# Edge messages of a graph layer: older messages summed in each two-pair turn, and gathers released at four points in eight units

## The chip, the cores and the metric

The kernel runs on one core of one Trainium2 chip. The metric is the device time of one execution in microseconds (us), and lower is better. A core has five engines with a queue each: TensorE (PE, matrix products; its weight loads are listed apart as PEld), VectorE (DVE), ScalarE (ACT), GpSimd (POOL) and SyncE (SP). Each engine works through its own list of instructions in order; where one needs another's result it waits for a semaphore. DMAs are started from the lists of SP, ACT and POOL.

## The reference

One layer of a graph network over 6,250 nodes with 256 features and 206,250 edges sorted by target node. Biases are left out here:

```python
h    = relu(layernorm(x))                      # node rows, 6250 x 256
e    = relu(raw @ W_e1.T) @ W_e2.T             # raw: 64 features of each edge
emb  = (e * (polarity + 0.01)) @ W_le.T
msg  = relu(h[src] + emb)                      # a gather of 256 floats for each edge
aggr = segment_sum(msg, dst)                   # sum over the edges of each target node
out  = x + relu(layernorm((h + aggr) @ W_g1.T)) @ W_g2.T
```

All of it is float32.

## The kernel before

Edges are cut into 403 blocks of 512. A block has two **units** of 256 edges, 806 in all (`NU`), and two blocks make a **pair** (`NP` = 202). `W_e2` and `W_le` are multiplied once at the start into one matrix `wc_s`, so an edge passes through two products. The steps of the edge loop, with the names and lines that the change touches:

- `first_layer(q)` (lines 278 to 311) takes pair `q`: four 64-row products of 512 columns (`pz<-raw,we_s`, line 292), two for each half `c` of the hidden features. The relu into `e1` is done by ACT (line 308, three of four) and DVE (line 305, one of four).
- `edge_part(u)` (317 to 334) takes unit `u`: four products (line 325) into one PSUM bank; DVE adds a bias and writes `msg` (line 331).
- `gather()` (627 to 639): POOL starts one indirect DMA for 128 source rows of `hb_d` into half of `hg[u]`, so there are two for each unit. There are 20 `hg` buffers (`HG`).
- `whole(u)` (677 to 690): DVE multiplies by the polarity and adds the gathered rows (line 685, two instructions), ACT does the relu (line 690). From here on `hg[u]` is a finished message; `made` counts them.
- `add_up(b)` (692 to 711): PE sums the messages of block `b` over target nodes with a 0/1 matrix `sel`, in four column strips of 32 (`pd<-hg,sel`, line 703). This frees the two `hg` buffers. `summed` counts pairs.

PSUM banks for the products come from a ring of seven (`Ring`). A product into a bank waits until the reader of what the bank held before has finished.

All engines' lists come from one Python loop that calls the steps in a fixed order (`manual_schedule`), so the order around the change is written out by hand. `forward(u)` (line 358) calls `edge_part(u)`, and after each fourth unit `turn_of` (343 to 356). In the middle of the run (`by_two`, pairs 6 to 195) only every second turn acts and does twice the work: that is the **two-pair turn** after unit 8k+1. It sums two pairs (`add_pairs`, 735), then does two `first_layer` calls and starts the loads of two more `raw` tiles. A period is thus eight units and one such turn; there are 93 full turns from unit 41 to unit 777.

Which pairs are summed is decided in `add_pairs`: a pair whose last message is older than the newest finished one, that is `4 * (summed + pairs) + 4 < made`. The first sum of a pair waits for that pair's last message (`newest`, lines 705 to 707). `whole` runs behind `edge_part` by a lag that falls by one every 44 units (`SHRINK`), from 18 to 1 (line 940). So the distance between the newest summed message and the newest finished one runs through 1, 2, 3 and 4 units as the lag falls; call this the **slack**. Over the run it is 1 or 2 in 45 of the 93 turns and 3 or 4 in the other 48.

Gathers are held back by a pace: `in_step` (646 to 652) is called after each unit and after each half of a first layer with the time that PE is assumed to need (1.754, 0.9; sums add 0.46 for a block, node work 0.81). It lets gathers go while their number times 1.288 is below the sum of these plus 6.0, and not more than the `hg` buffers allow (`4 * summed + HG` units). The first of those let go in a call waits for the PE instruction just recorded (`behind`); the others follow it in POOL's list. From unit 782 on (line 936) the gathers are only held by the buffers.

Finished nodes (128 at a time) go through the two last products, their layer norm and the output, as small steps (lines 159 to 232) spread over the units. The first of these in a node's life wait for sums that were written to DRAM and read back.

Of the kernel before, what the change touches and what calls it, by code (L numbers as in the profile page):

```python
# [36 lines left out]
NP = -(-NB // 2)  # L37
# [5 lines left out]
EDGE, LAYER, SUMS, NODES = 1.754, 0.9, 0.46, 0.81  # L43
STEP = 1.288
AFLOAT = 6.0
BANKS = 7
SHRINK = 44
RAW = 4
HG = 16 + RAW
FEW = 6  # L50
# [8 lines left out]
def group_of(b):  # L59
    return b // L  # L60
# [40 lines left out]
def gnn_kernel(ctx: ExitStack, tc: tile.TileContext, x, src_c, dst_c, dst_r, pol_c, raw_t, w_e1t, w_e2,  # L101
# [37 lines left out]
    def behind(ins, other):  # L139

        if other is not None:
            tc.add_manual_dep(ins.ins, other.ins.name, mybir.DependencyInfo(
                mybir.DependencyClass.Sync, mybir.DependencyReason.DATA), reason="one wait for several")
# [90 lines left out]
    NU = 2 * NB  # L234
    fast = ExitStack()
    fast.enter_context(tc.manual_schedule())
    with fast:
# [11 lines left out]

        banks = [psz.tile([P, 2, D], F32, name=f"pz{i}") for i in range(BANKS)]  # L250

        class Ring:
# [4 lines left out]
            def __call__(self):  # L257
                self.taken += 1
                return banks[self.taken % BANKS]

# [6 lines left out]
            def old(self):  # L267
                n = self.taken - BANKS
                return self.readers.get(n), self.writers.get(n)
# [8 lines left out]
        def first_layer(q):  # L278

            bs = [b for b in (2 * q, 2 * q + 1) if b < NB]  # L280
            if not bs:
                return
            for b in bs:
                e1[b] = e1_p.tile([P, 2, 512], F32, name="e1")
            pe, z = {}, {}
            for c in range(2):
                olds = []
                for s, b in enumerate(bs):
                    pe[s, c] = ps().rearrange("p a b -> p (a b)")
                    olds.append(ps.old())  # L290
                for s, b in enumerate(bs):
                    z[c] = nc.tensor.matmul(pe[s, c], we1_s[s * F:(s + 1) * F, c * P:(c + 1) * P],  # L292
                                            raw[q][s * F:(s + 1) * F, :], start=True, stop=True)
                    ps.wrote(z[c], len(bs) - 1 - s)
                    reader, writer = olds[s]
                    if reader is not None and writer is not None:
                        tc.declare_no_dep(z[c].ins, writer.ins, reason="the bank's reader has waited for it")
                    if s == 0:
                        for reader, _ in olds[1:]:
                            behind(z[c], reader)  # L300
                paced(LAYER, z[c])
            for c in range(2):
                for s, b in enumerate(bs):
                    if s == c == 1:
                        a = nc.vector.tensor_scalar(e1[b][:, c, :], pe[s, c], be1_s[:, c:c + 1], 0.0, op0=ALU.add,  # L305
                                                    op1=ALU.max)
                    else:
                        a = nc.scalar.activation(e1[b][:, c, :], pe[s, c], AF.Relu, bias=be1_s[:, c:c + 1])  # L308
                    behind(a, z[c])
                    ps.read(a, len(bs) * (1 - c) + len(bs) - 1 - s)  # L310
            raw.pop(q)

        def plain(u):

            return u < LEAD and u % 3 == 1

        def edge_part(u):

            nonlocal last_z
            b, v = divmod(u, 2)  # L320
            pz = ps()
            for i in range(2):
                k = (2 * v + i) * P
                for c in range(2):
                    last_z = nc.tensor.matmul(pz[:, i, :], e1[b][:, c, k:k + P], wc_s[:, c, :], start=c == 0, stop=c == 1)  # L325
            ps.wrote(last_z)
            msg[u] = msg_p.tile([P, 2, D], F32, name="msg")
            if plain(u):
                ps.read(nc.scalar.activation(msg[u], pz, AF.Copy))
            else:  # L330
                ps.read(nc.vector.tensor_add(msg[u], pz, bc_s))  # L331
            if v == 1:
                e1.pop(b)
            paced(EDGE, last_z)

        last_z = None
        sums = lambda last: None
        paced = lambda us, behind: None

        def by_two(q):  # L340
            return FEW <= q < NP - FEW
# [65 lines left out]
        with tc.tile_pool(name="p1", bufs=4) as p1, tc.tile_pool(name="p1x", bufs=11) as p1x:  # L407
# [76 lines left out]
            for k in range(len(parts) + 1):  # L484
                last = len(parts) - 1
# [20 lines left out]
                for _ in range((k > 0) + (k > 2 and k % 3 > 0)):  # L506
                    u = next(units, None)
# [37 lines left out]
        def rows_of_edges():  # L545
            nc.vector.tensor_tensor(
                rel[:, :full].rearrange("p (g k j) -> p g k j", k=L, j=S),
                dst_f[:, :full].rearrange("p (g k j) -> p g k j", k=L, j=S),
                base_b[:, :NF, :].rearrange("p g (o j) -> p g o j", o=1).to_broadcast([P, NF, L, S]), ALU.subtract)
            nc.vector.tensor_tensor(rel[:, full:], dst_f[:, full:], base_b[:, NF, :], ALU.subtract)  # L550
# [63 lines left out]
        with tc.tile_pool(name="hg", bufs=HG - RAW) as hg_p, tc.tile_pool(name="ms", bufs=4) as ms_p, \  # L614
# [5 lines left out]
            got = 2 * RAW  # L620
            acc = {}
            done = {}
            made = 0
            summed = 0
            spent = 0.0

            def gather(behind=None):

                nonlocal got
                u, i = divmod(got, 2)  # L630
                got += 1
                if i == 0:
                    hg[u] = (hx_p if u % HG < RAW else hg_p).tile([P, 2, D], F32, name="hg")
                g = nc.gpsimd.indirect_dma_start(  # L634
                    out=hg[u][:, i, :], out_offset=None, in_=hb_d,
                    in_offset=bass.IndirectOffsetOnAxis(ap=src_s[:, 2 * u + i:2 * u + i + 1], axis=0))
                if behind is not None:
                    tc.add_manual_dep(g.ins, behind.ins.name, mybir.DependencyInfo(
                        mybir.DependencyClass.Sync, mybir.DependencyReason.DATA), reason="gathers in step with PE")
# [3 lines left out]
                while got < 2 * min(NU, last):  # L643
                    gather()

            def in_step(us, behind):

                nonlocal spent
                spent += us
                while (got - 2 * RAW) * STEP < spent + AFLOAT and got < 2 * min(NU, 4 * summed + HG):  # L650
                    gather(behind)
                    behind = None

            def select(g):

                return [(g, lambda k=k: rows_of_block(g, k)) for k in range(len(blocks_of(g)))]
# [35 lines left out]
            def add_up(b, newest=()):  # L692

                nonlocal spent
                g = group_of(b)
                k = b - g * L
                if k == 0:
                    acc[g] = pd[:, g % 2, :] if g < NG - 1 else ps()[:, 0, :]
                    while rest and rest[0][0] <= g:
                        rest.popleft()[1]()  # L700
                for j in range(S):
                    m = hg[2 * b + j // 2]
                    z = nc.tensor.matmul(acc[g][j * W:(j + 1) * W, :], sel[g][:, k * S + j, :], m[:, j % 2, :],  # L703
                                         start=k == 0, stop=b == blocks_of(g)[-1])
                    if j == 0:
                        for other in newest:
                            behind(z, other)
                hg.pop(2 * b)
                hg.pop(2 * b + 1)
                spent += SUMS  # L710
                return g if b == blocks_of(g)[-1] else None
# [23 lines left out]
            def add_pairs(last=False):  # L735

                nonlocal summed
                whole_groups = []
                pairs = 0
                while summed + pairs < NP and min(4 * (summed + pairs) + 4, NU) < made + last:  # L740
                    pairs += 1
                for _ in range(pairs):
                    newest = done.get(4 * summed + 3, ())
                    for b in (2 * summed, 2 * summed + 1):
                        if b < NB:
                            whole_groups.append(add_up(b, newest))
                            newest = ()
                            if b % L == 0 and group_of(b) + 2 < NG:
                                rest.extend(select(group_of(b) + 2))
                    summed += 1  # L750

                for g in whole_groups:
                    keep(g)
# [160 lines left out]
            gathers(RAW + 1)  # L914
            sums = add_pairs
            paced = in_step
            def strips():
                rows_of_edges()
                rest.extend(select(0) + select(1))
# [44 lines left out]
            before, last = ending[-2], ending[-1]  # L964
# [201 lines left out]
```

## Time and profile before

| what | value |
|---|---|
| time, median of 3 runs | 2580.09 us (2572.7 to 2583.99) |
| the profiled execution: time, span | 2579.07 us, 2577.4 us |
| mean granted TensorE clock in it | 0.946 |
| PE busy | 2314.6 us, 90% of the span |
| PE weight loads busy | 1634.7 us, 63% |
| DVE busy | 1613.4 us, 63% |
| ACT busy | 1019.3 us, 40% |
| POOL busy | 1618.9 us, 63% |

The profile lists instructions in groups by source line and shape, as `line engine operation out<-in xcount | busy us, mean ns of one | idle us of the engine just before them, and what ended that idle time`. A product in float32 shows as two rows of PE and two of PEld. "issue" means that the profile shows nothing that the engine waited for; "remote" means a semaphore whose source it could not name. In rows of the waits the three numbers are the idle time in total, the number of times, and the longest, in us. In rows of time windows the columns are the length, then the busy time of PE, PEld, DVE, ACT and POOL with the number of instructions, the granted PE clock, the DMA engines' share and GB/s.

### The profile page before, as it was taken

The numbers are of one execution on the slowest core, as the hardware profiler recorded it, in microseconds if no ns is written. First come the engines' busy times: TensorE is split into PE (matmuls) and PEld (weight loads), VectorE is DVE, ScalarE is ACT, GpSimd is POOL, SyncE is SP. The second block draws the span as 40 slices with busy tenths as digits, with TensorE's granted clock in tenths as the row PEclk, the third lists the DMA queues.
The fourth block names the chain that finished last, engine by engine and source line by source line (L and its number), as shares of the span: only waits on it lengthen the run. The fifth ranks groups of instructions, "written<-read, shape, count | busy, mean of one in ns | idle before, by whom it ended". The sixth has DMA issues, their size and how long they took to land.

```text
span 2577.4 us, 36784 instructions
## 1 busy us (share of the span) xinstructions
PE 2314.6 (90%) x11940; PEld 1634.7 (63%) x11940; DVE 1613.4 (63%) x3705; ACT 1019.3 (40%) x1804; POOL 1618.9 (63%) x1675
## 2 busy tenths in 40 slices
PE   9988999989989998988888999998989899888968
PEld 6666666666657666666666666665667566666646
DVE  7866666666656665665656565665656566656636
ACT  7443434343334434343433333343434334333423
POOL 6666666666656666666666666666666666666661
PEclk9899999999989999999999999999999999999989
DMA  9443444434444434443444444444434445443441
GB/s 306 139 135 113 121 123 131 130 115 133 125 118 136 132 112 129 129 132 112 125 125 122 132 134 118 122 130 129 136 115 117 129 123 148 117 132 114 121 119 47
DMA packets 176430, 330.30 MB, mean 128 GB/s; under 512 B 39055, under 2 KB 98280, under 8 KB 176232
## 3 DMA queue, kind: packets, MB, share of 16 engines
q0 software_dynamic: 77376, 211.39, 29.2%
q1 hardware_dynamic: 97556, 113.22, 13.7%
q10 hardware_dynamic: 1300, 3.28, 0.4%
q8 instruction: 95, 1.56, 0.2%
q14 instruction: 103, 0.84, 0.1%
HBM read 293.92 MB, written 33.82 MB: 127 GB/s over the span
## 4 chain that ended last, share of the span: by engine, by line
PE 81%; issue 8%; DVE 5%; another core or an unknown queue 3%; ACT 3%; DMA 0%; ACTq 0%; DVEq 0%
PE pz L325 50%; PE pz L292 17%; PE pd L703 8%; DVE hg L685 2%; PE pz L181 2%; PE pz L212 2%; DVE msg L331 1%; ACT e L308 1%; ACT hg L690 1%; PE pz L166 0%; PE pz L199 0%; DVE st L151 0%; DVE sel L663 0%; ACT xt L440 0%
## 5 line engine op out<-in xcount | busy, mean ns | idle before, releaser
L634 POOL DMA_INDIRECT hg<-hb_d,src_s x1604 | 1574.1, 981 | 897.5 <-issue 520.0
L325 PE MATMUL pz<-wc_s,e 128*128 128x256 f32 x6448 | 1494.5, 388 | 15.5 <-issue 13.0
L325 PEld LDWEIGHTS pz<-wc_s,e 128*128 128x128 f32 x6448 | 1236.4, 194 | 281.6 <-ACT e L308 65.1
L690 ACT ACTIVATE hg<-hg 128x512 f32<-128x512 f32 x805 | 507.5, 630 | 988.5 <-DVE hg L685 800.8
L331 DVE TENSOR_TENSOR msg<-pz,bc_s 128x512 f32<-128x512 f32 x799 | 545.0, 684 | 404.9 <-remote 163.5
L685 DVE SCALAR_TENSOR_TENSOR hg<-msg,pol_s,hg 128x256 f32<-128x256 f32 x1612 | 694.7, 476 | 0.4
L292 PE MATMUL pz<-raw,we_s 64*128 64x512 f32 x1612 | 487.4, 696 | 141.6 <-ACT e L308 86.8
L305 DVE TENSOR_SCALAR e<-pz,vecs 128x512 f32<-128x512 f32 x201 | 150.8, 750 | 504.6 <-PE pz L292 358.4
L308 ACT ACTIVATE e<-pz,vecs 128x512 f32<-128x512 f32 x605 | 367.0, 692 | 202.3 <-PE pz L292 147.9
L292 PEld LDWEIGHTS pz<-raw,we_s 64*128 64x128 f32 x1612 | 177.0, 210 | 395.6 <-issue 232.8
L703 PE MATMUL pd<-hg,sel 128*32 128x256 f32 x3216 | 259.2, 388 | 88.1 <-issue 81.1
L703 PEld LDWEIGHTS pd<-hg,sel 128*32 128x32 f32 x3216 | 110.9, 109 | 216.6 <-issue 163.4
L718 ACT ACTIVATE ms<-pd 128x256 f32<-128x256 f32 x66 | 25.3, 383 | 318.8 <-remote 133.2
L663 DVE SCALAR_TENSOR_TENSOR sel<-iota_w,zero_c,rel 128x128 f32<-128x128 f32 x403 | 137.8, 342 | 0.0
L181 PE MATMUL pz<-wg_s,hT 128*128 128x256 f32 (+1 forms) x196 | 52.8, 393 | 2.6 <-ACT hg L690 2.1
L212 PE MATMUL pz<-wg_s,nT 128*128 128x256 f32 (+1 forms) x196 | 50.8, 382 | 2.0 <-ACT nT L203 1.8
L181 PEld LDWEIGHTS pz<-wg_s,hT 128*128 128x128 f32 (+1 forms) x196 | 37.7, 195 | 10.4 <-ACT hg L690 2.5
L212 PEld LDWEIGHTS pz<-wg_s,nT 128*128 128x128 f32 (+1 forms) x196 | 36.8, 190 | 8.7 <-ACT nT L203 2.7
L444 POOL TENSOR_TENSOR hb<-xt,rows_b 128x256 f32<-128x256 f32 (+1 forms) x49 | 34.1, 728 | 10.5 <-ACT xt L440 4.4
L203 ACT ACTIVATE nT<-pz,vecs 128x128 f32<-128x128 f32 (+1 forms) x98 | 38.7, 444 | 2.6 <-PE pz L199 2.4
L800 DVE TENSOR_TENSOR stb<-stb,ab 128x256 f32<-128x256 f32 x94 | 38.7, 411 | 0.0
L230 DVE SCALAR_TENSOR_TENSOR xt<-xt,zero_c,rows_b 128x128 f32<-128x128 f32 (+1 forms) x98 | 33.5, 343 | 0.0
(108 smaller groups left out, 376.2 us busy)
## 6 DMA issues: line engine op xcount, KB each, us to landing
raw<-in_raw_t_dram SPq DMA_DIRECT2D x202, 256.0 KB
hg<-hb_d,src_s POOLq DMA_INDIRECT x1604
sum_d<-zrow SPq DMA_DIRECT2D x94, 128.0 KB
ab<-sum_d SPq DMA_DIRECT2D x94, 128.0 KB
sum_d<-ms SPq DMA_DIRECT2D x264, 32.0 KB
hb_d<-hb SPq DMA_DIRECT2D x12, 512.0 KB
xt<-in_x_dram SPq DMA_DIRECT2D x48, 128.0 KB
out_dram<-ot SPq DMA_DIRECT2D x48, 128.0 KB
```

What stands on the lines that cost most here:

```text
L181: z = nc.tensor.matmul(ph[:n, 0, :], aT[:, c, :n], wg1_s[:, c, :], start=c == 0 and not bias_by_pe, stop=c == 1)
L212: z = nc.tensor.matmul(po[:n, 0, :], nT[:, c, :n], wg2_s[:, c, :], start=c == 0, stop=c == 1)
L292: z[c] = nc.tensor.matmul(pe[s, c], we1_s[s * F:(s + 1) * F, c * P:(c + 1) * P], raw[q][s * F:(s + 1) * F, :], start=True, stop=True)
L305: a = nc.vector.tensor_scalar(e1[b][:, c, :], pe[s, c], be1_s[:, c:c + 1], 0.0, op0=ALU.add, op1=ALU.max)
L308: a = nc.scalar.activation(e1[b][:, c, :], pe[s, c], AF.Relu, bias=be1_s[:, c:c + 1])
L325: last_z = nc.tensor.matmul(pz[:, i, :], e1[b][:, c, k:k + P], wc_s[:, c, :], start=c == 0, stop=c == 1)
L331: ps.read(nc.vector.tensor_add(msg[u], pz, bc_s))
L634: g = nc.gpsimd.indirect_dma_start(out=hg[u][:, i, :], out_offset=None, in_=hb_d, in_offset=bass.IndirectOffsetOnAxis(ap=src_s[:, 2 * u + ...
L663: nc.vector.scalar_tensor_tensor(sel[g][:, k * S:(k + 1) * S, :], iota_w.rearrange("p (o w) -> p o w", o=1).to_broadcast([P, S, W]), zero_ ...
L685: product = nc.vector.scalar_tensor_tensor(hg[u][:, i, :], m[:, i, :], pol_s[:, 2 * u + i:2 * u + i + 1], hg[u][:, i, :], op0=ALU.mult, op ...
L690: done[u] = product, nc.scalar.activation(hg[u], hg[u], AF.Relu)
L703: z = nc.tensor.matmul(acc[g][j * W:(j + 1) * W, :], sel[g][:, k * S + j, :], m[:, j % 2, :], start=k == 0, stop=b == blocks_of(g)[-1])
```

## The change

Two things change, both in the middle of the run.

**Sums.** `add_pairs` takes a pair only if it is two units older than before (`LATER`), except near the end and in the last call. The slack of 1, 2, 3, 4 units becomes 5, 6, 3, 4: in 45 of the 93 turns the pair summed second is the one that used to be summed first in the next place, so all sums there come one pair later; in the other 48 turns the same pairs are summed as before. A turn still has two pairs.

**Gathers.** `in_step` lets gathers go only when its caller says `gate`. That is so after units 3, 5 and 7 of eight, and after the first half of the first `first_layer` in the two-pair turn (the third of its eight products is then next). To the allowance half of half a period's assumed time is added (`HALF / 2`, 5.27). In the order of the built program a period's 16 gathers stand at four places, with some 5, 5, 3 and 3 or 4 gathers, where they stood at about eleven places with one or two each. In POOL's list 399 waits for PE are left of 1073, and 1074 separate wait instructions of 1424. PE's list has 407 separate wait instructions for 363. The other engines' work is the same and stands in the same order, but for what follows the sums.

Where the turns are not by two (the first gathers up to unit 24, and from unit 784) the gates stand at every first layer. One call before the loop lets the first gathers go.

```diff
+LATER = 2
+HALF = 4 * EDGE + 2 * LAYER + 2 * SUMS + NODES
...
-                paced(LAYER, z[c])
+                paced(LAYER, z[c], c == 0 and not (by_two(q - 2) and q % 2))
...
-            paced(EDGE, last_z)
+            paced(EDGE, last_z, by_two(u // 4) and u % 8 in (3, 5, 7))
...
-            def in_step(us, behind):
+            def in_step(us, behind, gate=False):
 
                 nonlocal spent
                 spent += us
-                while (got - 2 * RAW) * STEP < spent + AFLOAT and got < 2 * min(NU, 4 * summed + HG):
+                while gate and (got - 2 * RAW) * STEP < spent + AFLOAT + HALF / 2 and got < 2 * min(NU, 4 * summed + HG):
                     gather(behind)
                     behind = None
...
-                while summed + pairs < NP and min(4 * (summed + pairs) + 4, NU) < made + last:
+                while summed + pairs < NP and min(4 * (summed + pairs) + 4, NU) < made + last - (0 if last or summed > NP - 2 * FEW else LATER):
                     pairs += 1
...
             paced = in_step
+            in_step(0.0, None, True)
```

More of the change, by code (lines that the diff above doesn't have):

```diff
@@ L333, in edge_part @@
                 e1.pop(b)
-            paced(EDGE, last_z)
+            paced(EDGE, last_z, by_two(u // 4) and u % 8 in (3, 5, 7))
         last_z = None
         sums = lambda last: None
-        paced = lambda us, behind: None
+        paced = lambda us, behind, gate=False: None
         def by_two(q):
```

## The prediction

> **What bounds the kernel now.** I read the page's busy line and clock first, then the chain that ended last, the groups, the waits, and last time windows of the two-pair turns. In the first fence the reader is to see that PE leads, and that its clock dips now and then.
>
> ```profile
> span 2577.4 us, 36784 instructions
> ...
> PE 2314.6 (90%) x11940; PEld 1634.7 (63%) x11940; DVE 1613.4 (63%) x3705; ACT 1019.3 (40%) x1804; POOL 1618.9 (63%) x1675
> ...
> PEclk9899999999989999999999999999999999999989
> ...
> PE 81%; issue 8%; DVE 5%; another core or an unknown queue 3%; ACT 3%; DMA 0%; ACTq 0%; DVEq 0%
> ```
>
> The chain is PE for 81% and "issue" for 8%; POOL is not in it. The groups say where PE stands idle: 15.5 us before the 6448 rows of the units (L325), but 141.6 us before the first layers (L292) and 88.1 us before the sums (L703). The last two lie in the turns.
>
> ```profile
> L634 POOL DMA_INDIRECT hg<-hb_d,src_s x1604 | 1574.1, 981 | 897.5 <-issue 520.0 <-PE pz L325 79.8 <-PE pz L292 66.8
> L325 PE MATMUL pz<-wc_s,e 128*128 128x256 f32 x6448 | 1494.5, 388 | 15.5 <-issue 13.0 <-ACT msg L329 1.1 <-DVE xt L230 0.9
> ...
> L685 DVE SCALAR_TENSOR_TENSOR hg<-msg,pol_s,hg 128x256 f32<-128x256 f32 x1612 | 694.7, 476 | 0.4
> ...
> L331 DVE TENSOR_TENSOR msg<-pz,bc_s 128x512 f32<-128x512 f32 x799 | 545.0, 684 | 404.9 <-remote 163.5 <-PE pz L325 155.7 <-PE pz L181 37.1
> ...
> L292 PE MATMUL pz<-raw,we_s 64*128 64x512 f32 x1612 | 487.4, 696 | 141.6 <-ACT e L308 86.8 <-issue 44.8 <-DVE msg L331 6.7
> ...
> L703 PE MATMUL pd<-hg,sel 128*32 128x256 f32 x3216 | 259.2, 388 | 88.1 <-issue 81.1 <-ACT hg L690 5.2
> ```
>
> Now the turns. I cut each of the 93 as the stretch from the end of unit 8k+1's last product to the start of the next unit's first. First stand the shortest turn and a long one, then the sum rows of four groups, in this order: the 45 turns with slack 1 or 2; the 48 with slack 3 or 4; the 29 in which one or two gathers started within the turn's first 4 us; the 64 with three or four.
>
> ```profile
> 1044.79:1050.22 5.43, 5.43 (x49) 2.33 (x49) 2.30 (x4) 2.78 (x6) 3.58 (x4) 1.00 0.61 191
> 1212.36:1225.04 12.68, 9.39 (x48) 4.25 (x48) 6.02 (x13) 5.40 (x10) 7.05 (x9) 0.87 0.31 91
> ...
> sum 428.50, PE 325.32 PEld 128.10 DVE 166.83 ACT 152.18 POOL 251.12; mean PE 7.23 PEld 2.85 DVE 3.71 ACT 3.38 POOL 5.58
> ...
> sum 470.34, PE 352.88 PEld 135.69 DVE 167.54 ACT 165.75 POOL 276.14; mean PE 7.35 PEld 2.83 DVE 3.49 ACT 3.45 POOL 5.75
> ...
> sum 241.23, PE 194.49 PEld 80.22 DVE 85.35 ACT 86.96 POOL 131.30; mean PE 6.71 PEld 2.77 DVE 2.94 ACT 3.00 POOL 4.53
> ...
> sum 657.61, PE 483.71 PEld 183.57 DVE 249.02 ACT 230.97 POOL 395.96; mean PE 7.56 PEld 2.87 DVE 3.89 ACT 3.61 POOL 6.19
> ```
>
> A turn could take 5.43 us; the mean is (428.50 + 470.34) / 93 = 9.66. The 4.23 us between them, times 93, are 394 us: this is the only large sum that the change could touch.
>
> **Part 1, the sums.** What it removes is PE's wait for the newest message's relu:
>
> ```profile
> PE pd L703 <- issue: 81.1, 114, 1.9
> ...
> PEld pd L703 <- ACT hg L690: 8.6, 8, 3.0
> ```
>
> The two rows tell the sizes apart. The named wait is 8.6 us in 8 places in the whole run (the matmul row's 5.2 is the same wait seen later). The other 81.1 us of idle time in the sums, and 44.8 before the first layers, wait for nothing that the profile shows, and an older message does not end that. So the gain from the wait itself is at most 8.6 us. The other bound is from the groups. If later sums only turned turns with slack 1 or 2 into turns like those with slack 3 or 4, the mean would go from 428.50 / 45 = 9.52 to 470.34 / 48 = 9.80: 45 x 0.28 = 12.6 us worse. Why that can be: after the sums, the seventh of the eight products needs the bank that DVE's last `msg` (L331) still has to empty, so a PE that comes earlier waits there (L292 has 141.6 us of idle time, L703 88.1). The twelve turns with over 0.3 us between the two pairs' sums show it:
>
> ```profile
> sum 129.09, PE 90.64 PEld 35.05 DVE 59.16 ACT 45.07 POOL 78.72; mean PE 7.55 PEld 2.92 DVE 4.93 ACT 3.76 POOL 6.56
> ```
>
> They take 10.76 us with 3.20 of them idle; taking the named wait out (8.6 / 12 = 0.7) still leaves 10.0, above the mean of all turns. I take about half of the wait, -4 us: the row of the wait is the nearer one, since it is the removed thing itself, and part of it comes back at the banks. What else moves: the sums' buffers come free up to four units later in 45 turns, so gathers may be stopped by the buffers (rival 3); the copy of a finished group, its DMAs on SP and the node steps come one turn later in some places, on engines that are 40 to 63% busy: nothing. PE's list has 44 more wait instructions.
>
> ```profile
> L292 PEldq EVENT_SEMAPHORE  x247: 51/51/51, 4.5 to 2521.8; - x124
> ```
>
> At 51 ns each that is 2.2 us if none is hidden; they stand at the first layers, where PE waits for the same banks anyway, so 0 (kept as an end).
>
> One rule speaks on the clock. In the long turn, between 1212 and 1220, PE has no gap over 1.05 us, yet the clock is down after it:
>
> ```profile
> 1212.29 2.42 PE L703 MATMUL pd<-hg,sel 128*32 128x256 f32 x27
> 1215.74 0.38 PE L703 MATMUL pd<-hg,sel 128*32 128x256 f32 x1 [1.04 <-issue]
> 1216.47 0.39 PE L703 MATMUL pd<-hg,sel 128*32 128x256 f32 x1 [0.35 <-issue]
> 1217.91 0.63 PE L703 MATMUL pd<-hg,sel 128*32 128x256 f32 x3 [1.05 <-issue]
> ...
> 1212.00:1220.00 8.00, 4.71 (x37) 1.64 (x35) 5.63 (x13) 2.38 (x4) 5.49 (x6) 0.99 0.35 102
> 1220.00:1225.00 5.00, 5.00 (x15) 2.68 (x13) 0.75 (x1) 2.98 (x6) 1.89 (x2) 0.68 0.26 77
> ```
>
> The Trainium skill ("TensorE: Matmul & The Clock Gate", why this matters for your kernels) says that the clock halves after an idle gap of more than about 3 us; by that, removing waits of at most 3.0 us wins no clock and the sum stays at -4. The rows disagree in that 3.29 us of idle time scattered over 8 us were enough here. If each of the 8 waits cost one such dip, at 5 us x (1 - 0.68) = 1.6 us each, another 13 us would be won. I add nothing, because the scattered "issue" gaps, not the named waits, lead to the dip shown.
>
> **Part 2, the gates.** POOL's work stays: 1604 gathers at 981 ns plus some 0.3 us between them, 1.28 us each, 16 of them or 20.5 us in a period of about 25. Fewer waits (674 for PE, 350 wait instructions) shorten nothing: POOL is not in the chain. Nobody waits for gathered rows either: DVE's idle time before L685 is 0.4 us in the whole run. So no path is shorter or longer by itself, and the direct price is 0, covered by POOL's 897.5 us of idle time. What can change is when gathers run beside the turn, because turns beside many gathers are long: 241.23 / 29 = 8.32 us against 657.61 / 64 = 10.28. Both ends from there: every turn like the 29 gives 93 x (9.66 - 8.32) = -125 us; every turn like the 64 gives 93 x (10.28 - 9.66) = +58 us. Where do the gathers fall? Now they are let go singly up to unit 8k+1's end, and POOL, a little behind, carries two or three over. After the change: a unit takes PE 8 x 1494.5 / 6448 = 1.85 us, so from unit 3's gate to unit 7's there are 7.4 us and some node work, about 8, in which POOL has 5 + 3 gathers, 10 us: 2 us are left. At unit 7's end 3 or 4 more go, 4 to 5 us; units 0 and 1 take 3.7. So POOL is still busy for about 3 us of the turn: two starts, and the next gate, behind the sums and a quarter of the first layers (some 2 and 1 us of the shortest turn's 5.43), gives a third before 4 us. That is two to three, as before. I take 0 for the gates: nearest is the mixture that stands now.
>
> **Part 3, start and end.** The call before the loop lets the first gathers go some units sooner, beside other work: 0. From unit 782 on both kernels let all gathers go that the buffers allow, so the slow stretch there stays:
>
> ```profile
> 2471.00:2522.00 51.00, 33.30 (x138) 20.69 (x137) 19.98 (x51) 10.88 (x20) 32.63 (x35) 0.73 0.42 118
> ```
>
> **Sum.** The profiled execution took 2579.07 us, 1.7 more than its span and 1.0 less than the median of 2580.09. 2579.07 - 4 + 0 + 0 = 2575 us for it, and 2576 on the median's footing; I give 2575.
>
> **Rivals.**
> 1. Gates keep POOL out of the turn. If PE is held up in the sums, POOL runs dry until the next gate, which itself stands behind PE. For it: the 29 turns. Against: a short turn before leaves POOL behind, so a turn with few gathers may be short for another reason. Half of the -125 us: about 2515.
> 2. Slower: the group of unit 7's gate falls whole into the sums. The place is the first 4 us of the turn, the point at which it decides is POOL being 2 us more behind than I worked out, so that three or four gathers start there in every turn. For it: 8 gathers in 8 us from unit 3 on already need 10. Against: POOL's 4.5 us of slack in a period. +58 us: 2637.
> 3. Slower: buffers. In 45 turns sums come a pair later, the 20 `hg` buffers are full at unit 7's gate, and gathers wait for the turn. If each of these turns then has DVE wait for one gather of 1.28 us, that is +58 us, 2637. Against: 0.4 us of such waits now, and in the built order at least 2.5 units of gathers stand ahead of their use, more than before (1.5).
>    The Trainium skill ("DMA: Bandwidth & Descriptors", anatomy of one DMA) gives 2.0 us plus bytes / 436 GB/s for a plain DMA from this queue, an estimate of 2.3 us for a gather of 128 KB; no row here has the landing, and 2.5 units of 1.85 us would cover it.
> 4. The change does nothing that counts: 2579.
>
> **How the numbers follow.** Forecast with rival 4: 0.46, its own range 2558 to 2592. Rival 1: 0.26. Rival 2: 0.19. Rival 3: 0.09. Within 0.5% (12.9 us; about what a measurement of this kernel can tell, as its three runs lie within 11.3) are 0.32 of the 0.46; of the rest 0.10 is faster, since the forecast lies 5 us on that side and up to 17 more are open there (the rest of the wait, and its clock dips), and 0.04 is slower. Faster: 0.26 + 0.10 = 0.36; same 0.32; slower: 0.19 + 0.09 + 0.04 = 0.32. The range 2525 to 2625 holds the forecast and the milder part of each rival; about one in ten is left out at either end.
>
> **What would show it.** Right: waits of L703 for ACT hg gone, "issue" before L703 still near 80 us, L292's idle time up by a few us, mean turn 9.4 to 9.9 us, L685 idle near 0. Wrong: a mean turn under 9 with "issue" halved (rival 1), over 10 with a lower clock (rival 2), or DVE idle before L685 (rival 3). My weakest step is that the unexplained "issue" time stays, as I don't know its cause.

## The result, and the profile after

The changed kernel took 2690.27 us (median of 4 runs, 2680.63 to 2705.19) against 2580.06 us: a ratio of 1.0436 (of the mean times, as in all that follows), with a 95% interval of 1.0380 to 1.0491. The forecast was 2575 us with a range of 2525 to 2625. The kernel before takes 2541 to 2580 us in some series of runs and 2140 to 2142 us in others, on the same chips (two of the four that are known by number showed both), so every ratio here is taken within one series, and I call the two kinds **late** (2541 to 2580) and **prompt** (2140 to 2142). The measurement above is of the late kind.

The page of the changed kernel: the span, the engines, PE's clock by slices of time, and the chain that ended last.

```profile
span 2678.8 us, 36467 instructions
...
PE 2400.9 (90%) x11940; PEld 1653.4 (62%) x11940; DVE 1612.6 (60%) x3705; ACT 1020.9 (38%) x1804; POOL 1619.6 (60%) x1675
...
PEclk9999999898989999989999999999899999999999
...
PE 84%; issue 9%; DVE 4%; another core or an unknown queue 1%; ACT 1%; DMA 1%; SPq 0%; DVEq 0%; ACTq 0%
```

DVE, ACT and POOL are busy for as long as before; the span is 101.4 us longer. The groups (busy time, mean of one in ns, then the idle time before them and what ended it) say where:

```profile
L327 PE MATMUL pz<-wc_s,e 128*128 128x256 f32 x6448 | 1478.8, 385 | 17.4 <-issue 13.1 <-ACT msg L331 2.2 <-ACT e L310 1.1
...
L687 DVE SCALAR_TENSOR_TENSOR hg<-msg,pol_s,hg 128x256 f32<-128x256 f32 x1612 | 696.5, 479 | 0.4
L333 DVE TENSOR_TENSOR msg<-pz,bc_s 128x512 f32<-128x512 f32 x799 | 546.4, 686 | 557.0 <-remote 308.7 <-PE pz L327 180.6 <-PE pz L214 19.5
...
L294 PE MATMUL pz<-raw,we_s 64*128 64x512 f32 x1612 | 503.3, 710 | 63.4 <-issue 28.0 <-ACT e L310 25.4 <-DVE msg L333 4.0
L705 PE MATMUL pd<-hg,sel 128*32 128x256 f32 x3216 | 347.2, 407 | 178.2 <-issue 171.6 <-ACT hg L692 1.7
```

Busy and idle time together, the sums (L705, before L703) went from 259.2 + 88.1 = 347.3 to 525.4 us, the first layers (L294, before L292) from 629.0 to 566.7, the units' products (L327, before L325) from 1510.0 to 1496.2: +178 - 62 - 14 = +102 us. DVE still never waits for gathered rows (0.4 us before L687), but it stands idle longer before L333, where it takes PE's results: 557.0 us for 404.9 (the part put down to PE by name is 180.6 for 155.7, the part without a named source 308.7 for 163.5).

The same 93 windows of the two-pair turns as in the prediction, first all of them, then the 23 in which at most two gathers started in the first 4 us, then the other 70:

```profile
sum 1009.58, PE 779.55 PEld 298.86 DVE 352.11 ACT 319.50 POOL 499.42; mean PE 8.38 PEld 3.21 DVE 3.79 ACT 3.44 POOL 5.37
...
sum 225.57, PE 179.56 PEld 72.61 DVE 103.64 ACT 80.95 POOL 109.20; mean PE 7.81 PEld 3.16 DVE 4.51 ACT 3.52 POOL 4.75
...
sum 784.01, PE 599.99 PEld 226.25 DVE 248.47 ACT 238.56 POOL 390.22; mean PE 8.57 PEld 3.23 DVE 3.55 ACT 3.41 POOL 5.57
```

The turns took 428.50 + 470.34 = 898.84 us before and 1009.58 after: +110.7 us, which is more than the whole loss. A turn is 10.86 us for 9.66. Both groups are longer: 9.81 us for 8.32 in the first, 11.20 for 10.28 in the second.

PE's rows in one long turn show what such a turn is made of (start, length, idle time before it):

```profile
1374.57 0.39 PE L705 MATMUL pd<-hg,sel 128*32 128x256 f32 x1 [0.35 <-issue]
1376.66 0.38 PE L705 MATMUL pd<-hg,sel 128*32 128x256 f32 x1 [1.70 <-issue]
1377.38 0.38 PE L705 MATMUL pd<-hg,sel 128*32 128x256 f32 x1 [0.34 <-issue]
1378.08 0.39 PE L705 MATMUL pd<-hg,sel 128*32 128x256 f32 x1 [0.33 <-issue]
1379.49 1.93 PE L705 MATMUL pd<-hg,sel 128*32 128x256 f32 x11 [1.02 <-issue]
1381.35 2.97 PE L294 MATMUL pz<-raw,we_s 64*128 64x512 f32 x10
```

For some microseconds PE starts one product every 0.7 to 2.1 us and waits for nothing that the profile shows; then eleven come in 1.93 us. Taking as a slow stretch a chain of at least three PE products, each of which starts 0.56 to 0.90 us behind the one before, there are 30 of them with 45 us in the trace of before and 49 with 86 us in that of after.

### The profile page after: what moved, and what is told of

Same layout as the page of the kernel before. It is cut to its first block, busy times and chain, and to the rows that moved or that the text cites. A ratio compares the mean times of both kernels' runs of the same rounds, so it can differ in the third digit from the quotient of the medians.

```text
span 2678.8 us, 36467 instructions
## 1 busy us (share of the span) xinstructions
PE 2400.9 (90%) x11940; PEld 1653.4 (62%) x11940; DVE 1612.6 (60%) x3705; ACT 1020.9 (38%) x1804; POOL 1619.6 (60%) x1675
## 4 chain that ended last, share of the span: by engine, by line
PE 84%; issue 9%; DVE 4%; another core or an unknown queue 1%; ACT 1%; DMA 1%; SPq 0%; DVEq 0%; ACTq 0%
PE pz L327 51%; PE pz L294 17%; PE pd L705 12%; PE pz L214 2%; PE pz L183 2%; DVE hg L687 1%; DVE msg L333 1%; ACT e L310 1%; DMA xt<-in_x_dram 0%; PE pz L201 0%; PE pz L168 0%; SPq L421 0%; DVE stb L802 0%; SPq L278 0%
## 5 line engine op out<-in xcount | busy, mean ns | idle before, releaser
L327 PE MATMUL pz<-wc_s,e 128*128 128x256 f32 x6448 | 1478.8, 385 | 17.4 <-issue 13.1
L327 PEld LDWEIGHTS pz<-wc_s,e 128*128 128x128 f32 x6448 | 1220.7, 192 | 274.5 <-ACT e L310 58.0
L333 DVE TENSOR_TENSOR msg<-pz,bc_s 128x512 f32<-128x512 f32 x799 | 546.4, 686 | 557.0 <-remote 308.7
L687 DVE SCALAR_TENSOR_TENSOR hg<-msg,pol_s,hg 128x256 f32<-128x256 f32 x1612 | 696.5, 479 | 0.4
L294 PE MATMUL pz<-raw,we_s 64*128 64x512 f32 x1612 | 503.3, 710 | 63.4 <-issue 28.0
L705 PE MATMUL pd<-hg,sel 128*32 128x256 f32 x3216 | 347.2, 407 | 178.2 <-issue 171.6
L294 PEld LDWEIGHTS pz<-raw,we_s 64*128 64x128 f32 x1612 | 187.5, 221 | 340.6 <-issue 221.2
L705 PEld LDWEIGHTS pd<-hg,sel 128*32 128x32 f32 x3216 | 135.1, 112 | 363.2 <-issue 324.1
```

What stands on the lines that cost most here:

```text
L687: product = nc.vector.scalar_tensor_tensor(hg[u][:, i, :], m[:, i, :], pol_s[:, 2 * u + i:2 * u + i + 1], hg[u][:, i, :], op0=ALU.mult, op ...
```

## The experiments

The theories, in the order in which they came up. **A**: bunches of gathers beside the turn slow PE's sums. **B**: the loss comes with the later sums. **C**: the loss exists only in the late kind of series. **D**: only both parts together cost. **E**: gathers that follow each other on POOL without a pause hold up what PE does, the more the longer the row. **F**: not the rows, but how far ahead of PE the gathers run.

### The parts, first series (prompt)

Four edits of the changed kernel: gates undone; sums undone; no gate behind unit 8k+7; no `HALF / 2`.

```diff
 e1_later
-                while gate and (got - 2 * RAW) * STEP < spent + AFLOAT + HALF / 2 and ...
+                while (got - 2 * RAW) * STEP < spent + AFLOAT and ...
 e2_gates
-LATER = 2
+LATER = 0
 e3_no_gate7
-            paced(EDGE, last_z, by_two(u // 4) and u % 8 in (3, 5, 7))
+            paced(EDGE, last_z, by_two(u // 4) and u % 8 in (3, 5))
 e4_no_lead
-                while gate and (got - 2 * RAW) * STEP < spent + AFLOAT + HALF / 2 and ...
+                while gate and (got - 2 * RAW) * STEP < spent + AFLOAT and ...
```

> The later sums alone, with the gathers let go after every unit as before. Theory A (bunches of gathers at the turn slow PE's sums, and the later sums are harmless): 2560 to 2600 us, mean turn 9.4 to 9.9 us. Theory B (the loss comes with the later sums, which PE now enters without a wait): 2660 us or more, mean turn over 10.5 us.

> The gates alone, with LATER = 0. Theory A: 2660 to 2700 us, with the idle time before the sums near the 178 us of the changed kernel. Theory B: 2560 to 2600 us, idle time before the sums near 88 us.

> Later sums and gates, but no gate behind unit 8k+7: the gathers of that gate go with the turn's gate, behind the sums, so that POOL has finished its five or so gathers of unit 5's gate (6.4 us) before the turn, four units (7.4 us) later. Theory A: the turn gets shorter than in either kernel, 7.4 to 9.7 us, and the time is 2400 to 2580 us, unless DVE then waits for gathers. Theory B: 2670 to 2710 us as in the changed kernel.

> Later sums and gates, without the HALF / 2 of 5.3 us by which the gathers are ahead: the same four gates and the same number behind each in the long run, but about four gathers fewer in flight or held. Theory A: 2650 to 2710 us, because as many gathers start at the turn. Theory B: the same, so this run tells whether the lead itself matters: if the lead is the cause, 2560 to 2620 us.

Measured, with the kernel before at 2141.88 us: 2141.15, 2140.81, 2141.82 and 2147.47 us, ratios 1.0005, 1.0000, 1.0001 (each within 0.0013) and 1.0020 (1.0007 to 1.0033). No theory had expected that. There are no slow stretches in these traces, the clock is 0.996 to 0.998, and no variant differs by over 0.2%: nothing is told apart, except that this series does not show the effect at all. The traces show why the gates have nothing to hold back here: from 100 us on POOL runs its gathers as one row without a pause, in the later sums alone (which has the old pace) as in the kernels with gates (in the one without the lead there are two such rows).

### The changed kernel again, second series (prompt)

> The changed kernel again, unedited. On another chip the four variants had no slow turn at all: 2141 to 2147 us like the kernel before, clock 0.997, no idle time before the sums. Theory C (the loss of 110 us is how the chip of the first measurement, whose PE falls into stretches of one instruction per 0.70 us, answers the change; a chip without these stretches shows none of it): on a chip where the kernel before takes about 2141 us, 2136 to 2148 us and a ratio of 0.997 to 1.003; on one where it takes about 2580 us, 2680 to 2705 us. Theory D (the two parts together cost what neither does alone): 4% over the kernel before on any chip.

> The later sums alone again, for a chip where the kernel before takes about 2580 us. There, theory A (bunches of gathers at the turn): 2560 to 2600 us; theory B (the later sums): 2660 us or more. On a chip where the kernel before takes 2141 us: 2136 to 2148 us and nothing is told apart.

> The gates alone again, with LATER = 0. Where the kernel before takes about 2580 us, theory A: 2660 to 2700 us; theory B: 2560 to 2600 us. Where it takes 2141 us: 2136 to 2148 us.

With the kernel before at 2140.96 us: the changed kernel 2136.61 us, ratio 0.9970 (0.9955 to 0.9984); later sums alone 0.9989 (0.9976 to 1.0001); gates alone 0.9993 (0.9983 to 1.0003). D, which was to hold on any chip, falls: both parts together cost nothing here, if anything they win 0.3%. C stands. Here the groups do what the code says. First the gates alone, then the changed kernel (its page's engine line, then three groups):

```profile
L294 PE MATMUL pz<-raw,we_s 64*128 64x512 f32 x1612 | 383.7, 608 | 16.4 <-ACT e L310 8.1 <-DVE msg L333 7.0 <-DMA raw<-in_raw_t_dram 1.2
L705 PE MATMUL pd<-hg,sel 128*32 128x256 f32 x3216 | 195.5, 382 | 6.8 <-ACT hg L692 6.8
```

```profile
PE 2103.5 (98%) x11940; PEld 1560.1 (73%) x11940; DVE 1623.5 (76%) x3705; ACT 1010.8 (47%) x1804; POOL 1612.7 (75%) x1675
...
L294 PE MATMUL pz<-raw,we_s 64*128 64x512 f32 x1612 | 384.6, 609 | 22.9 <-ACT e L310 12.5 <-DVE msg L333 7.7 <-DMA raw<-in_raw_t_dram 1.4
L705 PE MATMUL pd<-hg,sel 128*32 128x256 f32 x3216 | 194.5, 382 | 0.3 <-ACT hg L692 0.3
...
L687 DVE SCALAR_TENSOR_TENSOR hg<-msg,pol_s,hg 128x256 f32<-128x256 f32 x1612 | 722.6, 479 | 255.1 <-DMA hg<-hb_d,src_s 250.9
```

The later sums take PE's wait for the newest relu from 6.8 to 0.3 us, and the first layers' idle time grows from 16.4 to 22.9: the 6.5 us come back at the banks to the tenth. PE is at 98%, and that DVE waits 255.1 us for gathers costs nothing.

### More and less pace, third series (late)

Both from `LATER = 0`: one with no pace at all (a gather waits only for its buffer), one with two gates in eight units and eight gathers at each.

```diff
 e5_free
-                while gate and (got - 2 * RAW) * STEP < spent + AFLOAT + HALF / 2 and got < ...:
-                    gather(behind)
+                while got < 2 * min(NU, 4 * summed + HG):
+                    gather(None)
 e6_two_gates
-                paced(LAYER, z[c], c == 0 and not (by_two(q - 2) and q % 2))
+                paced(LAYER, z[c], c == 0 and not by_two(q - 2))
-            paced(EDGE, last_z, by_two(u // 4) and u % 8 in (3, 5, 7))
+            paced(EDGE, last_z, by_two(u // 4) and u % 8 in (3, 7))
-                while ... < spent + AFLOAT + HALF / 2 and ...
+                while ... < spent + AFLOAT + HALF and ...
```

> The kernel before with no step between gathers and PE at all: POOL starts each gather as soon as its buffer is free. Theory C (the gathers' pace costs time only on a chip whose PE has the stretches of 0.70 us per instruction): where the kernel before takes about 2141 us, 2120 to 2150 us, and DVE's idle time before its products falls well below the 250 us of the other variants, because the gathers land earlier. Where it takes about 2580 us: theory A (gathers beside the turn slow PE) 2640 us or more; theory B (the later sums) 2540 to 2620 us.

> The gates alone (LATER = 0) and coarser: eight gathers at a time behind units 8k+3 and 8k+7, ahead by HALF. Where the kernel before takes about 2141 us, theory C: 2130 to 2160 us, at most 1% more, since POOL has 490 us of idle time. Where it takes about 2580 us: theory A 2680 us or more; theory B 2560 to 2610 us.

With the kernel before at 2576.92 us: 3266.45 us, ratio 1.2685 (1.2651 to 1.2720), and 3338.69 us, 1.2962 (1.2915 to 1.3010). The size was not expected by anyone. A had given "2640 us or more" and "2680 us or more", so its sign holds; B, whose later sums are in neither kernel, falls as the only cause. But A's place, the turn, is not where the free gathers lose. The turns' windows, first of the free gathers, then of the two gates:

```profile
sum 550.29, PE 523.47 PEld 213.56 DVE 321.76 ACT 288.78 POOL 335.32; mean PE 5.63 PEld 2.30 DVE 3.46 ACT 3.11 POOL 3.61
```

```profile
sum 1681.76, PE 1109.98 PEld 374.94 DVE 284.55 ACT 305.28 POOL 700.81; mean PE 11.94 PEld 4.03 DVE 3.06 ACT 3.28 POOL 7.54
```

With two gates a turn takes 1681.76 / 93 = 18.08 us, but with free gathers 550.29 / 93 = 5.92, near the shortest that there is, in a kernel that loses 690 us. Its loss is in the units: 446.5 us of idle time before L327, and 1740.1 us of busy time there for 1494.5 before, at a mean granted clock of 0.848 for 0.946. One period of it, first PE, then DVE's first message in it, then the first and the last of the 16 gathers that POOL runs without a pause:

```profile
842.21 6.31 PE L327 MATMUL pz<-wc_s,e 128*128 128x256 f32 x28
848.89 0.38 PE L327 MATMUL pz<-wc_s,e 128*128 128x256 f32 x1 [0.36 <-issue]
...
851.04 0.46 PE L327 MATMUL pz<-wc_s,e 128*128 128x256 f32 x1 [1.03 <-issue]
853.14 0.38 PE L327 MATMUL pz<-wc_s,e 128*128 128x256 f32 x1 [1.64 <-issue]
855.26 0.59 PE L327 MATMUL pz<-wc_s,e 128*128 128x256 f32 x1 [1.74 <-issue]
857.36 0.58 PE L327 MATMUL pz<-wc_s,e 128*128 128x256 f32 x1 [1.51 <-issue]
859.44 1.01 PE L327 MATMUL pz<-wc_s,e 128*128 128x256 f32 x2 [1.50 <-issue]
860.84 7.92 PE L327 MATMUL pz<-wc_s,e 128*128 128x256 f32 x28 [0.39 <-issue]
```

```profile
860.94 0.69 DVE L333 TENSOR_TENSOR msg<-pz,bc_s 128x512 f32<-128x512 f32 x1 [6.85 <-issue]
...
862.34 0.68 DVE L333 TENSOR_TENSOR msg<-pz,bc_s 128x512 f32<-128x512 f32 x1
```

```profile
838.09 0.95 POOL L636 DMA_INDIRECT hg<-hb_d,src_s  x1 [11.10 <-ACT hg L692]
839.34 0.95 POOL L636 DMA_INDIRECT hg<-hb_d,src_s  x1 [0.30 <-issue]
...
856.91 0.94 POOL L636 DMA_INDIRECT hg<-hb_d,src_s  x1 [0.30 <-issue]
870.07 0.94 POOL L636 DMA_INDIRECT hg<-hb_d,src_s  x1 [12.21 <-issue]
```

The row of gathers runs from 838.1 to 857.9. PE's records go on at full pace until 848.5, then products come one by one, at last one per 2.1 us or so, until 859.4, and from 860.8 it is back to 28 products in 7.9 us. The granted clock is 1.00 from 842.2 to 848.5, 0.73 from there to 860.8 and 0.78 in the 28 products behind it, so the slow clock comes after the stall and adds to it. Stranger: the first unit of the period is finished at 842.21 + 8 x 6.31 / 28 = 844.0 by PE's records, but DVE gets it at 860.94, 17 us later and 3 us behind the end of the row; then five messages follow at DVE's own pace of 1.4 us. So in this period PE's results are held up first and PE itself after that, while a long row of gathers runs. From here theory E.

I counted the rows in each trace (gathers that start less than 0.45 us behind the end of the one before; the first 100 us left out):

```
late series             rows   gathers in one   ratio in its series
before (first series)    278        5.7          1
changed (first series)   204        7.7          1.0436
free gathers              97       16.2          1.2685
two gates                113       13.9          1.2962
```

And what DVE waits for a unit's result behind PE's recorded end of it, over the units from 42 on for which it stood idle over 0.15 us, by how POOL stood at that end (mean, and the number of units; idle is more than 0.45 us behind a row):

```
                       POOL idle       1st to 7th gather   8th gather of a row, or later
before                 0.12 us (14)     2.65 us (181)       4.32 us (21)
changed, late          1.30 us (9)      3.15 us (156)       6.27 us (59)
free gathers           0.04 us (23)    10.74 us (143)      12.09 us (42)
two gates              0.09 us (15)     3.28 us (144)      10.66 us (106)
changed, prompt        none             none                0.09 us (19)
```

The last line is the changed kernel of the second series: there POOL runs nearly the whole loop as one row, and PE's results are never late. So a long row alone does not hold up PE; it takes the late kind of series too.

Where in a row does PE stand idle with nothing that it is seen to wait for ("issue")? From 100 us to unit 778, idle time over 0.2 us in one place, and in brackets the time that POOL spent in that part of its rows, all in us:

```
                       gather 1 to 6   gather 7 to 9   10 or later    within 3 us behind   later
before                 15 (1585)       44 (335)          9 (47)        55 (384)             0 (9)
changed, late          22 (1343)       22 (374)         86 (253)       73 (373)             0 (123)
free gathers            6 (712)         5 (356)        413 (877)       92 (254)             1 (855)
two gates              17 (820)         3 (359)        421 (773)       93 (277)             0 (899)
```

In all four, PE is hardly ever stalled beside the first six gathers of a row, for the largest share of the time beside the tenth and later ones and just behind the row, and next to never when POOL has paused for over 3 us. That speaks for E and against F: the gathers are furthest ahead of PE when a row has just ended, and 3 us later PE runs freely. The mean time from a gather's end on POOL to its use by DVE (gathers 100 to 1540) does not order the losses either: 14.2 us before, 16.2 in the changed kernel, 48.2 with free gathers, but only 23.9 with two gates, which lose most.

### The parts again, fourth series (late)

The kernels of `e2_gates` and `e1_later`, and the kernel before with `AFLOAT` halved.

```diff
 e7_lead3
-AFLOAT = 6.0
+AFLOAT = 3.0
```

> The gates alone (LATER = 0). Theory E (where the kernel before takes about 2577 us, POOL's gathers that follow each other without a pause hold up PE's signals, about 1 us for each gather beyond the fifth of such a row, and the gates make the rows longer, 7.7 gathers on average for 5.7): 2660 to 2710 us there, rows of 7 or more gathers. Theory B (the later sums are the cause): 2560 to 2600 us. Where the kernel before takes 2141 us: 2135 to 2148 us.

> The later sums alone. Theory E: where the kernel before takes about 2577 us, 2555 to 2600 us, rows of 5.5 to 6 gathers as before. Theory B: 2660 us or more. Where the kernel before takes 2141 us: 2135 to 2148 us.

> The kernel before with AFLOAT = 3.0 for 6.0, nothing else: every gather is let go 3 us (two gathers) later, so POOL runs into its wait for PE sooner and the rows get shorter. Theory E: where the kernel before takes about 2577 us, 2450 to 2560 us and rows under 5.5 gathers; theory B says nothing of it (2560 to 2600 us). Where the kernel before takes 2141 us, DVE waits for gathers for more than the 250 us of the others, and it is 2140 to 2190 us.

With the kernel before at 2540.94 us: the gates alone 2628.18 us, 1.0359 (1.0322 to 1.0397); the later sums alone 2541.69 us, 1.0009 (0.9989 to 1.0028); less lead 2539.33 us, 1.0010 (0.9990 to 1.0029). Their rows: 8.0, 5.8 and 6.1 gathers. This settles the parts, each taken alone: the gates are the loss, the later sums cost nothing, and B falls. The changed kernel itself was not in this series, so whether the later sums add something beside the gates (1.0436 there, 1.0359 here, with intervals that just overlap) was not measured. Less lead did not shorten the rows, against what E had me expect of it, and the time did not change either, though a gather's end lay 10.2 us ahead of its use for 12.8 in the later sums alone; F, too, would have had less lead help. The sums and first layers, gates alone, then later sums alone:

```profile
L294 PE MATMUL pz<-raw,we_s 64*128 64x512 f32 x1612 | 475.4, 700 | 65.3 <-ACT e L310 34.4 <-issue 15.3 <-DVE msg L333 7.6
L705 PE MATMUL pd<-hg,sel 128*32 128x256 f32 x3216 | 324.2, 404 | 178.2 <-issue 164.3 <-ACT hg L692 10.0
```

```profile
L294 PE MATMUL pz<-raw,we_s 64*128 64x512 f32 x1612 | 486.0, 678 | 160.1 <-ACT e L310 106.0 <-issue 30.4 <-DVE e L307 10.6
L705 PE MATMUL pd<-hg,sel 128*32 128x256 f32 x3216 | 232.2, 385 | 37.3 <-issue 35.9
```

The idle time before the sums is 178.2 us in the gates alone and 37.3 in the later sums alone, in one series, so it belongs to the gates (that the changed kernel of the first series has the same 178.2 to the digit is chance).

### Pauses in the rows, fifth and sixth series (both prompt)

Two small sums on POOL behind every fourth gather, added to the free gathers, the changed kernel and the kernel before.

```diff
+    pause = const.tile([P, P], F32, name="pause")
...
+                if got > 100 and got % 4 == 0:
+                    for i in range(2):
+                        nc.gpsimd.tensor_add(pause, bc_s[:, 0, :P], bc_s[:, 1, :P])
```

> The kernel with free gathers (27% slower than before) and nothing but a pause added: two small sums on POOL (about 0.8 us, 401 times, some 320 us of POOL time) behind every fourth gather, which break the rows of 16 gathers into rows of 4. Theory E (it is the length of the row without a pause that holds up PE's signals): on a chip where the kernel before takes about 2540 to 2580 us, 2380 to 2650 us instead of 3266. Theory F (it is that gathers run far ahead of PE, or how many run beside certain units, and the pauses do not matter): 3100 us or more. Where the kernel before takes 2141 us, POOL becomes the bound at 1604 x 1.28 + 320 = 2373 us plus the start: 2370 to 2450 us.

> The changed kernel with the same pause behind every fourth gather. Theory E: where the kernel before takes about 2540 to 2580 us, the gates' loss of 90 to 110 us is gone and the time is 2380 to 2580 us. Theory F: 2640 us or more. Where the kernel before takes 2141 us: 2370 to 2450 us, POOL-bound.

> The kernel before with the same pause. Theory E: rows of 5.7 gathers become rows of at most 4 and the time falls to 2380 to 2520 us where the kernel before takes 2540 to 2580 us, unless a pause of 0.8 us is too short to let PE's signals out. Theory F: 2540 to 2620 us. Where the kernel before takes 2141 us: 2370 to 2450 us.

> Free gathers with the pause behind every fourth, again, for a chip in the state of the first measurement. On one where the kernel before takes 2140 us it took 2523 us (POOL-bound, pauses of 0.97 us). Theory E: where the kernel before takes 2540 to 2580 us, 2520 to 2700 us. Theory F: 3100 us or more. Where the kernel before takes 2140 us: 2515 to 2530 us.

> The changed kernel with the pause, again. Theory E: where the kernel before takes 2540 to 2580 us, 2520 to 2610 us. Theory F: 2640 us or more. Where the kernel before takes 2140 us: 2510 to 2525 us.

> The changed kernel without the gate behind unit 8k+7, again: three gates in eight units, five or more gathers at each. Where the kernel before takes 2540 to 2580 us: theory E, the rows are as long as with four gates or longer, 2650 us or more; theory A (it is the gathers beside the turn), 2400 to 2580 us. Where it takes 2140 us: 2136 to 2148 us.

With the kernel before at 2139.66 us: 2523.46, 2517.57 and 2518.10 us (1.1799, 1.1769, 1.1763). With it at 2141.38 us, the free gathers again 2524.74 us, the changed kernel with pauses 2516.43 us, and the one without the gate at unit 7 2142.42 us (0.9999, 0.9986 to 1.0012). Both series were prompt, so rows broken by pauses were not measured where the loss shows: this stays open. In a prompt series the pauses only make POOL the bound, and a little later than I had worked out (2370 to 2450 us): a sum took 483 ns, and DVE waits for gathers, here with free gathers:

```profile
L691 DVE SCALAR_TENSOR_TENSOR hg<-msg,pol_s,hg 128x256 f32<-128x256 f32 x1612 | 830.4, 534 | 559.6 <-DMA hg<-hb_d,src_s 553.1
...
L645 POOL TENSOR_TENSOR pause<-bc_s 128x128 f32<-128x128 f32 x756 | 364.8, 483 | 36.2
```

No version was found that beats both kernels in both kinds of series.

## Why the prediction was wrong

- **What bounds the kernel.** Right in place: PE leads, and the only large sum that the change could touch was the 394 us of excess in the turns. All of the loss, 110.7 us, lies there.
- **Part 1, the sums: -4 us.** The mechanism was right, the size was off: the named wait goes (5.2 to 1.7 us in the matmul row; 6.8 to 0.3 in the second series), and in the rows of the second series all of it, not half, comes back at the banks. Measured alone: +0.09% of 2541 us, 2 us, with an interval of -3 to +7, so -4 lies just outside. The end of +12.6 us for later sums is excluded.
- **Part 2, the gates: 0 us, with ends of -125 and +58.** This is the step that failed: "the direct price is 0, covered by POOL's 897.5 us of idle time". Alone the gates cost 2628.18 - 2540.94 = 87 us, beyond the end of +58 that I had worked out. Two sentences of it are wrong. The one is "Fewer waits (674 for PE, 350 wait instructions) shorten nothing: POOL is not in the chain." The waits for PE are what cut POOL's rows into pieces; with 399 of 1073 left, a row grew from 5.7 to 7.7 gathers, the time that POOL spent in the tenth or a later gather of a row from 47 to 253 us, and PE's idle time in it from 9 to 86 us. The other is the measure by which I set the ends, the gathers that start in the first 4 us of a turn: the share of turns with three or more went only from 64 to 70 of 93, but turns of both groups got longer by 0.9 to 1.5 us. So the number of starts inside the turn is not what sets its length; how long the row already is when PE gets there fits better.
- **Part 3, start and end: 0.** Nothing in the runs speaks against it: outside the turns the changed kernel is 101.4 - 110.7 = -9 us.
- **Rival 2** had the right sign and too small a price, by the wrong point: it put the cost into gathers that start in the sums. With free gathers the slow stretch goes where the row of gathers goes (turns of 5.92 us, 446.5 us of idle time in the units).
- **Rival 3** did not happen: 0.4 us before L687. In the prompt series DVE does wait for gathers, 250 us and more, and it costs nothing because PE is at 98%.
- **Rival 1** is excluded by the sign.
- **What would show it.** Of the marks that I gave, the mean turn over 10 us came (10.86), with a clock of 0.942 for 0.946; the idle time before the first layers did not go up a little but fell from 141.6 to 63.4 us, which a PE that arrives there later would explain. The step that I had called my weakest, that the "issue" time stays, broke with it: 81.1 us before the sums became 171.6.
- **The rule on the clock** decides nothing here: the mean clock hardly moved (0.942 for 0.946).

What stays open: by what way the gathers hold PE up, why only some series show it, and whether the length of a row is the cause or goes along with something else (for instance how many gathers are still under way). For the row speak the timeline above, the place of PE's idle time in the rows, and the table of rows and ratios, in which long rows and large losses go together (though the two longest are not in order); rows broken by pauses were measured in prompt series only.

## What to carry to other kernels

When a profile has idle time that waits for nothing it shows, ask which other engine was busy just then, and do not price an edit of that engine's list at zero because the engine is off the chain: here the waits that looked superfluous on POOL were the pauses behind which PE ran freely. Time a change in more than one series, with the kernel before in each: the same edit was -0.3% in one and +4.4% in another. Where a late series is possible, one or two gathers to a wait, as in the kernel before, are the safer choice of those measured, and in the prompt series that cost 0.3% at most; pauses made of extra work on POOL cost 18% there.

## What the runs showed of the hardware

- One program takes 2141 or 2577 us on the same chip, depending on the series. In the late kind, PE's result reaches DVE 17 us after PE's recorded end in the period shown, and 25 us after it at most (free gathers); with POOL idle, 0.04 to 0.12 us after it on average in three of four kernels. The Trainium skill ("Perfetto Trace Analysis", Tensor Engine Instruction) says that PE's end in a profile is estimated from the instruction's size, not observed, and that the signal comes after it. The traces agree: a long delay behind PE's end can be PE itself or its signal, and these records can't say which.
- The stall does not begin with a slower PE clock. In the period shown PE's records have full pace while the row is young, at a granted clock of 1.00: 28 products in 6.31 us at 842.21, 0.225 us each, where the units of the prompt changed kernel take 1456.1 / 6448 = 0.226.
- DVE's products take longer beside sums on POOL than beside gathers: 534 ns on average with the pauses, 479 in the changed kernel of the second series, where POOL's gathers run nearly without a pause. The Trainium skill ("GPSIMD Engine Reference", Specifications) says that POOL shares its SBUF interfaces with DVE, with contention for DVE instructions that have two SBUF inputs, as these products have; the 11% here agree.
- A gather's landing, which no row had shown for the prediction, stands in the page of the changed kernel with pauses: 2.8 us, for the 2.3 us that was worked out from the Trainium skill ("DMA: Bandwidth & Descriptors", anatomy of one DMA). The measurement decides.

```profile
hg<-hb_d,src_s POOLq DMA_INDIRECT x1604, 2.8
```
